# Layer 1 of a two-layer kernel: the experts' weighted biases for four token tiles at once, on four 32-row parts of TensorE

## The chip, the cores and the metric

The kernel runs on one core of one Trainium2 chip. The metric is the time of one execution in device microseconds (us). A core has five engines that work side by side, each through its own queue of instructions: TensorE (PE, with its weight loads listed as PEld), VectorE (DVE), ScalarE (ACT), GpSimd (POOL), and SyncE (SP), which here only starts DMA transfers. They hand work to each other through semaphores. Matmul results land in PSUM, eight banks of 128 partitions by 512 fp32 numbers, from which DVE and ACT read them; everything else lies in SBUF.

## The reference, cut to what matters

Eight sequences of 512 tokens with 256 features go through two layers. Layer 0 (a recurrent attention and a mixture of experts that takes one expert per token) isn't touched by the change. Layer 1 is a softmax attention with 16 heads, then a mixture in which every token goes through all eight experts:

```python
gate_logits = jax.nn.softmax(x @ gate_w + gate_b, axis=-1)
selected = (gate_logits >= THRESHOLD).astype(x.dtype)
weights = gate_logits * selected
wsum = jnp.sum(weights, axis=-1, keepdims=True)
weights = weights / jnp.where(wsum == 0, jnp.ones_like(wsum), wsum)
for e in range(E):
    out = out + weights[:, e:e + 1] * (x @ expert_w[e] + expert_b[e])
```

The sum over `e` of `weights[:, e] * expert_b[e]` is a small matrix product by itself: the weights of a token (8 numbers) times the table of biases (8 by 256). This is the "weighted bias" of which the change speaks. The result, times a gate row, is added to `x`.

## The kernel before, in words

Layer 1 works batch by batch. A batch has NT = 4 token tiles of 128 tokens. The main loop of layer 1 counts steps `n`, 16 per batch: four groups of heads (`c`) times four query tiles (`i`). A step does three things for attention. `scores` makes the scores of four heads: four matmuls on 32 rows each, each into a PSUM bank of its own (line 1419); VectorE adds the position bias and takes the lowest value (line 1428), ScalarE takes the exponential (line 1433). `turn`, four steps behind, transposes the probabilities of four heads through TensorE (line 1445) and copies them back, two with VectorE (line 1454) and two with ScalarE (line 1452). `weigh`, one step further behind, multiplies them with the values (line 1466), adding up in one bank that is held for four steps.

All else is cut into pieces that are put into a list `side` with a place each, counted in steps, and are issued between the steps when their place has come. `prologue` (the norm of the next batch, its transposes on line 179 and its projections, lines 240 and 257) and `tail` (all that follows attention for the batch before) make such pieces. A `tail` begins six steps into the next batch. Its pieces, with their places counted from there: `heads_out`, `heads_T`, `project` (lines 1492, 1507, 1518) for the four tiles, then `statistics` at 6.6, the transposed norm and the gate's logits (line 1542) from 7.6, `weights` at 14 (the softmax over eight gates and the threshold, for all four tiles in one go), `weights_T` at 15.4, and `experts(i)` at 17, 18.9, 20.8 and 22.7. The tail of a batch thus reaches into the second batch after it. The last tile of the last batch but one is put off to 30.8, into the tail of the last batch.

`weights_T` transposes the weights of the four tiles (128 by 8 each) with four transposes into one bank (line 1576), and VectorE copies the 8 by 512 result into `wT` (line 1578). `experts(i)` starts with the weighted bias of its tile: one matmul with 8 rows (line 1584; an fp32 matmul shows as two instructions in the trace), copied by ScalarE into the accumulator `acc` (line 1586). Then come four pairs of experts, two fp32 matmuls into one bank for each pair (line 1590, sixteen instructions in all), from which VectorE adds `weight * result` to `acc`, expert by expert (line 1595). GpSimd multiplies with the gate row (line 1599; VectorE in the last batch) and starts the DMA that adds `acc` to the output (line 1600).

What is issued in what order: the pieces stand in the order in which the loop traces them, and the framework's planner places them at compile time. In the program before, TensorE's order in layer 1 is that of tracing but for four instructions out of some three thousand, which a later one passed because their input was not ready in the planner's reckoning; on VectorE and ScalarE it mixes more freely. `tc.issue_after(step)` keeps `turn`, `weigh` and the side pieces behind the step's score matmuls on TensorE. At run time each engine goes through its queue in that order and waits where an input or a buffer isn't ready. A PSUM tile gets the bank that was released longest ago; with one of the eight banks held by `weigh`, seven go round.

In SBUF the pool `layer1` ends at byte 115,328 of a partition and the next one in use begins at 116,800. The table of biases, `eb`, is loaded by SP in layer 0, in `load1`.

Of the kernel before, what the change touches and what calls it, by code (L numbers as in the profile page):

```python
# [11 lines left out]
F32 = mybir.dt.float32  # L12
U32 = mybir.dt.uint32
AF = mybir.ActivationFunctionType
ALU = mybir.AluOpType
# [4 lines left out]
P = 128  # L20
B = 8
S = 512
D = 256
NH = 16
HD = 16
NT = S // P
NE = 8
# [36 lines left out]
def tile_two_layers(ctx: ExitStack, tc: tile.TileContext, t: dict, out: bass.AP):  # L64
    nc = tc.nc
# [9 lines left out]
    def bank():  # L75
        n_ps[0] += 1
        return banks[0].tile([P, 512], F32, tag="ps", name=f"ps{n_ps[0]}")
# [17 lines left out]
    ident = cst[:, C_ID : C_ID + P]  # L95
# [57 lines left out]
    w1 = {}  # L153
# [124 lines left out]
    with ExitStack() as l0:  # L278
# [988 lines left out]
        def follow(i, qk, V):  # L1267


            x1, norms = [], []  # L1270
            _, pieces = attend(i, qk, V, x1, norms)
            work = {}

            def begin():
                work["route"] = route(i, x1, norms)
                next(work["route"])

            def more():
                next(work["route"])

            def settle():
                work["experts"] = experts(i, *next(work["route"]))
                next(work["experts"])

            def on():
                next(work["experts"])

            pieces += [(34, begin), (42, more), (51, more), (57, more), (60, more), (62, settle)]

            late, pace, starts = {  # L1290
                NT - 1: (0, 4, [10 * j for j in range(NSLOT)]),
                NT - 2: (14, 4.2, [43]),
                NT - 3: (11, 4.6, [8, 22, 37, 47]),
            }.get(i, (11, 4.6, [8, 22, 37, 47]))
            rest = []
            for j in range(NSLOT):
                for half in range(2):
                    if j < late:
                        pieces.append((68 + pace * (j + half / 2), on))
                    else:  # L1300
                        rest.append((starts[j - late] + 3 * half, on))
            if i == NT - 1:
                rest += [(200, on), (250, on)]

            at, apart = [(1, 2.2), (21, 2.2), (108, 7), (0, 0)][i]
            return pieces, rest, [
                (at + apart * n, on) for n in range(B + DEPTH[i])
            ]

        def load1():  # L1310

            early.close()
            wp1 = ctx.enter_context(tc.tile_pool(name="weights1", bufs=1, side="right"))

            def put(key, shape, src):
                w1[key] = wp1.tile(shape, F32, name=f"{key}1")
                nc.sync.dma_start(w1[key], src)

            put("wqkv", [P, 2, 3 * D], t["W_attnT"].rearrange("(k p) m -> p k m", p=P))
            put("bqk", [P, 4], t["b_qk"])  # L1320
            put("bv", [P, D], t["b_v"].partition_broadcast(P))
            w1["strips"] = wp1.tile([P, NH, S], F32, name="strips1")
            put("wp", [P, 2, D], t["W_projT"].rearrange("(k p) m -> p k m", p=P))
            put("bp", [P, D], t["b_proj"].partition_broadcast(P))
            put("gw", [P, 2, NE], t["gate_w1"].rearrange("(k p) e -> p k e", p=P))
            put("gbias", [P, NE], t["gate_b1"].partition_broadcast(P))
            put("eb", [NE, D], t["expert_b"])

            w1["xs"] = wp1.tile([P, NT, D], F32, name="xs_first")

# [26 lines left out]
        for i in range(NT):  # L1357
# [23 lines left out]
            if i + 1 < NT:  # L1381
                parts, more, _ = front(i + 1, 47 if i > 0 else 30)
                pieces = pieces + more + (later if i == 0 else [])
            run(pieces, scan(i, before["K"], before["V"]))
        more, last, _ = follow(NT - 1, before["qk"], before["V"])
# [18 lines left out]
    with ExitStack() as l1:  # L1404
        lp = l1.enter_context(tc.tile_pool(name="layer1", bufs=2))

        strips, wp, bp = (w1[key] for key in ("strips", "wp", "bp"))
        gw, gbias, eb, ew = (w1[key] for key in ("gw", "gbias", "eb", "ew"))

        def scores(b, c, i):  # L1410


            kT, qT, prs = got[b]["kT"], got[b]["qT"], got[b].setdefault(c, {})
            g, o = c // 2, c % 2
            W = (i + 1) * P
            pscs = [bank() for _ in range(4)]
            for r in range(4):
                rows = slice(32 * r, 32 * r + 32)
                made = nc.tensor.matmul(  # L1419
                    pscs[r][:, :W], qT[rows, g, o, i * P : (i + 1) * P], kT[rows, g, :W],  # L1420
                    start=True, stop=True,
                )
            for r in range(4):
                n = 8 * g + 2 * r + o

                sc = lp.tile([P, S], F32, tag="sc", name=f"sc{b}_{i}_{n}", bufs=4)
                low = lp.tile([P, 1], F32, tag="low", name=f"low{b}_{i}_{n}", bufs=8)
                nc.vector.tensor_tensor_reduce(  # L1428
                    out=sc[:, :W], in0=pscs[r][:, :W], in1=strips[:, n, S - W :],
                    scale=1.0, scalar=3.0e38, op0=ALU.add, op1=ALU.min, accum_out=low,  # L1430
                )
                pr = lp.tile([P, W], F32, tag=f"pr{i}", name=f"pr{b}_{i}_{n}", bufs=6)
                nc.scalar.activation(pr, sc[:, :W], AF.Exp, bias=low, scale=-1.0)  # L1433
                prs[r, i] = pr
            return made.ins
# [40 lines left out]
        def tail(b, got):  # L1476
# [3 lines left out]
            g11 = spread(lp, "g11", b)  # L1480
            hT = []
            lg = lp.tile([P, NT, NE], F32, tag="lgd", name=f"lgd{b}")
            wt = lp.tile([P, NT, NE], F32, tag="wtd", name=f"wtd{b}")

            ys, yTt, stats, wTs = {}, {}, {}, []

            def heads_out(i):

# [59 lines left out]
            def weights():  # L1548
                def row4(name):
                    return lp.tile([P, NT], F32, tag=name, name=f"{name}{b}")  # L1550

                def wide(x):
                    return x.unsqueeze(2).to_broadcast([P, NT, NE])

                top = row4("topd")
                nc.vector.tensor_reduce(top, lg, AX.X, ALU.max)
                nc.vector.tensor_sub(lg, lg, wide(top))
                nc.scalar.activation(lg, lg, AF.Exp)
                tot = row4("totd")
                nc.vector.tensor_reduce(tot, lg, AX.X, ALU.add)  # L1560
                nc.vector.reciprocal(tot, tot)
                nc.vector.tensor_mul(lg, lg, wide(tot))
                nc.vector.scalar_tensor_tensor(
                    wt.rearrange("p i e -> p (i e)"), lg.rearrange("p i e -> p (i e)"), 0.1,
                    lg.rearrange("p i e -> p (i e)"), ALU.is_ge, ALU.mult,
                )
                ws = row4("wsd")
                nc.vector.tensor_reduce(ws, wt, AX.X, ALU.add)
                nc.vector.scalar_tensor_tensor(ws, ws, 0.0, ws, ALU.is_equal, ALU.add)
                nc.vector.reciprocal(ws, ws)  # L1570
                nc.vector.tensor_mul(wt, wt, wide(ws))

            def weights_T():
                pt = bank()
                for i in range(NT):
                    nc.tensor.transpose(pt[:NE, i * P : (i + 1) * P], wt[:, i, :], ident)
                wT = lp.tile([NE, S], F32, tag="wT", name=f"wT{b}", bufs=1)
                nc.vector.tensor_copy(wT, pt[:NE, :])
                wTs.append(wT)

            def experts(i):
                cols = slice(i * P, (i + 1) * P)
                pb = bank()
                nc.tensor.matmul(pb[:, :D], wTs[0][:, cols], eb, start=True, stop=True)  # L1584
                acc = lp.tile([P, D], F32, tag="accd", name=f"accd{b}_{i}")
                nc.scalar.copy(acc, pb[:, :D])
                for e in range(0, NE, 2):
                    pe = bank()
                    for k in range(2):
                        nc.tensor.matmul(  # L1590
                            pe, hT[0][:, k, cols], ew[:, k, e : e + 2, :],
                            start=(k == 0), stop=(k == 1),
                        )
                    for j in range(2):
                        nc.vector.scalar_tensor_tensor(  # L1595
                            acc, pe[:, j * D : (j + 1) * D], wt[:, i, e + j : e + j + 1], acc,
                            ALU.mult, ALU.add,
                        )
                (nc.vector if b == B - 1 else nc.gpsimd).tensor_mul(acc, acc, g11)  # L1599
                nc.gpsimd.dma_start(y2d[b][i], acc, accum_op=ALU.add)  # L1600
# [21 lines left out]
        for n in range(B * STEP + NT + 1):  # L1622
            b, m = divmod(n, STEP)
# [23 lines left out]
            with tc.issue_after(step):  # L1647
                last, turned = turned, None
                if NT <= n < B * STEP + NT:
                    b, m = divmod(n - NT, STEP)  # L1650
# [110 lines left out]
```

## Time and profile before

| what | us |
|---|---|
| median of 3 runs (lowest, highest) | 2216.25 (2212.28, 2221.45) |
| the profiled execution, and its span from first to last instruction | 2215.8, 2214.1 |
| TensorE busy (share of the span) | 1718.3 (78%) |
| VectorE busy | 1580.6 (71%) |
| ScalarE busy | 1081.1 (49%) |
| GpSimd busy | 642.1 (29%) |
| bias matmuls, line 1584: 64 instructions, busy | 23.0 |
| expert matmuls, line 1590: 512 instructions, busy | 232.6 |
| weight transposes, line 1576: 32 instructions of 0.27 each | first at 1518.7, last at 2175.9 |
| copies of the bias into the accumulator, line 1586: 32, mean | 0.37 |
| copy of the transposed weights, line 1578: 8, mean | 0.68 |
| mean granted TensorE clock over the span (1 is full speed) | 0.874 |

Layer 0 fills the span to about 1360 us, layer 1 the rest. Busy times of matmuls overlap, since several are in the array at once: where it matters what a group of matmuls costs, the distance from its first issue to the issue of the next group says more than the duration of its instructions.

### The profile page before, as it was taken

How to read it: one execution, taken by the hardware profiler on the slowest of the kernel's cores; microseconds unless marked ns; L12 is line 12 of the kernel's file. 1: busy time of each engine (PE TensorE's matmuls, PEld its weight loads, DVE VectorE, ACT ScalarE, POOL GpSimd, SP SyncE). 2: the span in 40 equal slices, each digit the busy share in tenths (PEclk: the TensorE clock that was granted, in tenths of full speed). 3: DMA queues.
4: the chain of work that ended last, by engine and by line, in shares of the span. 5: the costliest groups of instructions: out<-in, count | busy, mean ns of one | idle time of the engine just before them, and what ended most of it. 6: DMA issues, size and time to landing. Idle time of an engine off the chain costs nothing. (4 is left out here: it accounts for less than half of the span.)

```text
span 2214.1 us, 32513 instructions
## 1 busy us (share of the span) xinstructions
PE 1718.3 (78%) x10906; PEld 1196.4 (54%) x10906; DVE 1580.6 (71%) x4523; ACT 1081.1 (49%) x2674; POOL 642.1 (29%) x920
## 2 busy tenths in 40 slices
PE   5342056479686796839995898999999999999988
PEld 4221035259574695728874786555555555555544
DVE  5999998969989699899753004677676666676754
ACT  4253035555366553623342336886666574747421
POOL 1313013355254553543463643010111101010210
PEclk8666566689897898969997999999999999999998
DMA  5110000358103582128765883000101010000101
GB/s 165 49 50 5 0 1 11 99 209 313 33 13 108 198 311 72 38 90 303 234 110 153 272 275 72 1 20 8 27 13 25 13 22 13 22 20 6 23 17 12
DMA packets 88630, 189.58 MB, mean 86 GB/s; under 512 B 13688, under 2 KB 67104, under 8 KB 75664
## 3 DMA queue, kind: packets, MB, share of 16 engines
q0 software_dynamic: 33696, 137.43, 19.3%
q1 hardware_dynamic: 54768, 50.09, 7.9%
q8 instruction: 86, 1.41, 0.3%
q14 instruction: 80, 0.66, 0.1%
HBM read 175.10 MB, written 36.93 MB: 96 GB/s over the span
## 5 line engine op out<-in xcount | busy, mean ns | idle before, releaser
L1433 ACT ACTIVATE pr<-sc,low 128x384 f32<-128x384 f32 (+3 forms) x512 | 255.6, 556 | 196.3 <-DVE low L1428 193.2
L1428 DVE CUSTOM_DVE_ANT_0 sc<-ps,strips 128x384 f32<-128x384 f32 (+3 forms) x512 | 225.6, 486 | 87.2 <-PE ps L1419 55.6
L1190 PE MATMUL ps<-hTs,w 128*128 128x128 f32 x1920 | 239.4, 286 | 14.0 <-DMA w<-in_wrows,idx 9.0
L1190 PEld LDWEIGHTS ps<-hTs,w 128*128 128x128 f32 x1920 | 235.5, 201 | 21.4 <-issue 11.6
L745 DVE TENSOR_REDUCE state<-terms 128x16 f32<-128x272 f32 x512 | 227.3, 444 | 15.6
L756 DVE TENSOR_TENSOR state<-state,upd 128x256 f32<-128x256 f32 x511 | 222.2, 435 | 14.9
L1590 PE MATMUL ps<-ew,hTd 128*128 128x512 f32 x512 | 232.6, 608 | 0.0
L1209 PE MATMUL ps<-w,act 128*128 128x256 f32 x960 | 223.7, 387 | 6.5 <-DMA w<-in_wrows,idx 4.0
L741 DVE TENSOR_TENSOR terms<-state,K 128x256 f32<-128x256 f32 x512 | 216.3, 422 | 14.9
L751 DVE TENSOR_TENSOR upd<-K,state 128x256 f32<-128x256 f32 x511 | 214.4, 420 | 16.1
L1199 ACT ACTIVATE act<-ps,w 128x128 f32<-128x128 f32 x480 | 137.3, 370 | 135.4 <-PE ps L1190 122.2
L1445 PE MATMUL ps<-cst,pr 128*128 128x128 f32 x1280 | 189.9, 292 | 15.3 <-DVE low L1428 12.0
L1209 PEld LDWEIGHTS ps<-w,act 128*128 128x128 f32 x960 | 182.0, 195 | 31.4 <-issue 4.0
L1595 DVE SCALAR_TENSOR_TENSOR accd<-ps,wtd,accd 128x256 f32<-128x256 f32 x256 | 123.7, 483 | 100.7 <-PE ps L1590 86.6
L1445 PEld LDWEIGHTS ps<-cst,pr 128*128 128x128 f32 x1280 | 147.2, 147 | 84.8 <-DVE low L1428 24.1
L1599 POOL TENSOR_TENSOR accd<-accd,bc_g 128x256 f32<-128x256 f32 x28 | 20.4, 728 | 545.6 <-DVE accd L1595 545.6
L1145 POOL DMA_INDIRECT w<-in_wrows,idx x120 | 124.2, 1035 | 184.1 <-ACT act L1199 58.8
L1590 PEld LDWEIGHTS ps<-ew,hTd 128*128 128x128 f32 x512 | 96.3, 193 | 120.5 <-issue 106.4
L1419 PE MATMUL ps<-kT,qTc 32*128 32x128 f32 (+3 forms) x1024 | 132.1, 491 | 4.4 <-DVE low L1428 2.6
L1454 DVE COPY prT<-ps 128x512 f32<-128x512 f32 (+3 forms) x256 | 117.0, 484 | 8.9 <-PE ps L1445 8.5
L1452 ACT COPY prT<-ps 128x512 f32<-128x512 f32 (+3 forms) x256 | 98.9, 414 | 7.2 <-PE ps L1445 6.6
L1165 PE MATMUL ps<-cst,hslot 128*128 128x128 f32 x120 | 24.7, 290 | 98.2 <-DMA hslot<-hs 71.3
(296 smaller groups left out, 2956.3 us busy)
## 6 DMA issues: line engine op xcount, KB each, us to landing
hs<-zero SPq DMA_DIRECT2D x4, 1920.0 KB
hslot<-hs SPq DMA_DIRECT2D x60, 128.0 KB
ys<-ysb POOLq DMA_DIRECT2D x60, 128.0 KB
x<-in_x SPq DMA_DIRECT2D x32, 128.0 KB
strips<-strip_d SPq DMA_DIRECT2D x16, 256.0 KB
out<-accd POOLq DMA_DIRECT2D x32, 128.0 KB
wm<-in_wmod SPq DMA_DIRECT2D x4, 768.0 KB
xt<-in_x SPq DMA_DIRECT2D x12, 256.0 KB
```

The source lines that it names most:

```text
L741: nc.vector.tensor_mul(term[:, :, :HD], M, K[:, s, :].unsqueeze(1).to_broadcast([P, HD, HD]))
L745: nc.vector.tensor_reduce(delta, term, AX.X, ALU.add)
L751: nc.vector.tensor_mul(upd, K[:, s, :].unsqueeze(2).to_broadcast([P, HD, HD]), delta.unsqueeze(1).to_broadcast([P, HD, HD]),)
L756: yield nc.vector.tensor_sub(M, M, upd).ins
L1190: nc.tensor.matmul(ph[:, q * P : (q + 1) * P], w[:, k * FF + f * P : k * FF + (f + 1) * P], hT[:, k, :], start=(k == 0), stop=(k == 1),)
L1199: nc.scalar.activation(act[:, f, :], ph[:, q * P : (q + 1) * P], AF.Relu, bias=w[:, 2 * FF + f : 2 * FF + f + 1],)
L1209: nc.tensor.matmul(py[:, :D], act[:, f, :], w[:, f * D : (f + 1) * D], start=(f == 0), stop=(f == NFC - 1),)
L1419: made = nc.tensor.matmul(pscs[r][:, :W], qT[rows, g, o, i * P : (i + 1) * P], kT[rows, g, :W], start=True, stop=True,)
L1428: nc.vector.tensor_tensor_reduce(out=sc[:, :W], in0=pscs[r][:, :W], in1=strips[:, n, S - W :], scale=1.0, scalar=3.0e38, op0=ALU.add, op1= ...
L1433: nc.scalar.activation(pr, sc[:, :W], AF.Exp, bias=low, scale=-1.0)
L1445: nc.tensor.transpose(pt[:, (i - j) * P : (i - j + 1) * P], prs[r, i][:, j * P : (j + 1) * P], ident,)
L1590: nc.tensor.matmul(pe, hT[0][:, k, cols], ew[:, k, e : e + 2, :], start=(k == 0), stop=(k == 1),)
```

## The change

The four tiles' weights now lie in one tile of SBUF of 128 tokens by 4 by 32, tile `i` in columns 32i to 32i+7, the other columns zero. There are two such tiles, used in turn by even and odd batches; GpSimd sets them to zero once, at the beginning of layer 1. One transpose of the whole 128 by 128 square puts tile `i`'s weights on partitions 32i to 32i+7. The table of biases is loaded four times, onto the same partitions. The four bias matmuls then read four different 32-row parts of the array and write four banks; they and ScalarE's four copies into accumulators move from `experts` into `weights_T`, so that a batch's four accumulators exist from there on (four slots instead of two). The two operations of `weights` that worked on flat rows of 32 numbers now work on 4 by 8 numbers at a stride of 32; their element counts are the same.

```diff
-            put("eb", [NE, D], t["expert_b"])
+            w1["eb"] = wp1.tile([P, D], F32, name="eb1")
+            for i in range(NT):
+                nc.sync.dma_start(w1["eb"][32 * i : 32 * i + NE, :], t["expert_b"])
...
+        wts = []
+        for k in range(2):
+            wts.append(lp.tile([P, NT, 32], F32, name=f"wtd{k}", bufs=1))
+            nc.gpsimd.memset(wts[k], 0.0)
...
-            wt = lp.tile([P, NT, NE], F32, tag="wtd", name=f"wtd{b}")
+            wt = wts[b % 2][:, :, :NE]
...
-                nc.vector.scalar_tensor_tensor(
-                    wt.rearrange("p i e -> p (i e)"), lg.rearrange("p i e -> p (i e)"), 0.1,
-                    lg.rearrange("p i e -> p (i e)"), ALU.is_ge, ALU.mult,
-                )
+                nc.vector.scalar_tensor_tensor(wt, lg, 0.1, lg, ALU.is_ge, ALU.mult)
...
             def weights_T():
                 pt = bank()
+                nc.tensor.transpose(
+                    pt[:, :P], wts[b % 2].rearrange("p i e -> p (i e)"), ident
+                )
+                wT = lp.tile([P, P], F32, tag="wT", name=f"wT{b}", bufs=1)
+                nc.vector.tensor_copy(wT, pt[:, :P])
+                pbs = [bank() for _ in range(NT)]
                 for i in range(NT):
-                    nc.tensor.transpose(pt[:NE, i * P : (i + 1) * P], wt[:, i, :], ident)
-                wT = lp.tile([NE, S], F32, tag="wT", name=f"wT{b}", bufs=1)
-                nc.vector.tensor_copy(wT, pt[:NE, :])
-                wTs.append(wT)
+                    rows = slice(32 * i, 32 * i + NE)
+                    nc.tensor.matmul(
+                        pbs[i][:, :D], wT[rows, :], eb[rows, :], start=True, stop=True
+                    )
+                for i in range(NT):
+                    acc = lp.tile([P, D], F32, tag="accd", name=f"accd{b}_{i}", bufs=4)
+                    nc.scalar.copy(acc, pbs[i][:, :D])
+                    accs.append(acc)
 
             def experts(i):
                 cols = slice(i * P, (i + 1) * P)
-                pb = bank()
-                nc.tensor.matmul(pb[:, :D], wTs[0][:, cols], eb, start=True, stop=True)
-                acc = lp.tile([P, D], F32, tag="accd", name=f"accd{b}_{i}")
-                nc.scalar.copy(acc, pb[:, :D])
+                acc = accs[i]
                 for e in range(0, NE, 2):
```

More of the change, by code (lines that the diff above doesn't have):

```diff
@@ L1482, in tail @@
             lg = lp.tile([P, NT, NE], F32, tag="lgd", name=f"lgd{b}")
-            wt = lp.tile([P, NT, NE], F32, tag="wtd", name=f"wtd{b}")
-            ys, yTt, stats, wTs = {}, {}, {}, []
+            wt = wts[b % 2][:, :, :NE]
+            ys, yTt, stats, accs = {}, {}, {}, []
             def heads_out(i):
```

## The prediction

> **What bounds the kernel now.** I read the page first, for the shape of the run. TensorE's row climbs to 9s in the right third; that is layer 1, the only place the change touches.
>
> ```profile
> PE   5342056479686796839995898999999999999988
> ```
>
> Then busy time by stretch, one stretch per batch of layer 1, cut at the first weight transpose of each batch (columns: length, then busy us and count of PE, PEld, DVE, ACT, POOL, then the granted clock).
>
> ```profile
> 1727.00:1832.50 105.50, 103.26 (x600) 56.77 (x596) 71.06 (x248) 64.16 (x142) 12.23 (x16) 0.97 0.09 18
> 1936.20:2037.80 101.60, 100.39 (x601) 54.89 (x598) 68.99 (x238) 60.53 (x137) 12.25 (x16) 1.00 0.07 14
> ```
>
> TensorE is busy 98% of a batch, VectorE 67%, ScalarE 61%. Equal work took 101.6 us at clock 1.00 and 105.5 at 0.97: throttling is worth up to 4 us a batch, and comes and goes.
>
> "Busy" does not say that a removed matmul shortens anything, so I took the timeline of the weight loads, which shows when each group is issued (columns: start, length, line, tiles, form, count, idle time before it and who ended it).
>
> ```profile
> 1726.97 0.31 PEld L1576 LDWEIGHTS ps<-cst,wtd 128*8 128x8 f32 x4 [0.84 <-DVE prT L1454]
> 1727.50 0.31 PEld L1419 LDWEIGHTS ps<-kT,qTc 32*128 32x128 f32 x8 [0.22 <-DVE prT L1454]
> ...
> 1731.61 0.29 PEld L1419 LDWEIGHTS ps<-kT,qTc 32*128 32x128 f32 x2 [0.36 <-ACT prT L1452]
> ...
> 1733.81 0.29 PEld L1584 LDWEIGHTS ps<-eb,wT 8*128 8x128 f32 x2 [0.41 <-DVE low L1428]
> 1734.43 0.30 PEld L1590 LDWEIGHTS ps<-ew,hTd 128*128 128x128 f32 x2 [0.33 <-DVE low L1428]
> ...
> 1745.77 0.36 PEld L1507 LDWEIGHTS ps<-cst,yc 128*128 128x128 f32 x2
> 1746.10 0.47 PEld L1492 LDWEIGHTS ps<-cst,yTc 128*128 128x128 f32 x4
> 1746.73 0.29 PEld L1584 LDWEIGHTS ps<-eb,wT 8*128 8x128 f32 x2 [0.17 <-ACT xnc L172]
> 1747.36 0.30 PEld L1590 LDWEIGHTS ps<-ew,hTd 128*128 128x128 f32 x2 [0.33 <-DVE rinvc L1495]
> ...
> 1754.42 0.31 PEld L1419 LDWEIGHTS ps<-kT,qTc 32*128 32x128 f32 x8 [0.76 <-DVE accd L1595]
> 1755.06 1.29 PEld L1445 LDWEIGHTS ps<-cst,pr 128*128 128x128 f32 x12 [0.33 <-issue]
> ...
> 1764.98 0.36 PEld L1507 LDWEIGHTS ps<-cst,yc 128*128 128x128 f32 x2
> 1765.51 0.29 PEld L1584 LDWEIGHTS ps<-eb,wT 8*128 8x128 f32 x2 [0.17 <-issue]
> ```
>
> A bias matmul (L1584) holds the issue for 0.62 us (1746.73 to 1747.36) and the interval is the same in every batch of the loop: it waits for nothing. The eight loads of a score step (four heads on 32 rows each, two passes, 128x256) take 0.64 us (1754.42 to 1755.06), no more than the two of one bias. And two 128x128 transposes take 0.33 us before another group of that form (1745.77 to 1746.10) but 0.53 before a bias (1764.98 to 1765.51): the change of form costs 0.2 more.
>
> The end of the kernel has experts alone:
>
> ```profile
> 2184.61 0.69 PE L1584 MATMUL ps<-eb,wT 8*128 8x256 f32 x2
> 2185.24 7.13 PE L1590 MATMUL ps<-ew,hTd 128*128 128x512 f32 x16
> 2192.30 0.69 PE L1584 MATMUL ps<-eb,wT 8*128 8x256 f32 x2
> ```
>
> A tile there lasts 7.69 us, of which sixteen expert matmuls at their spacing of 0.43 are 6.83; the bias costs 0.86 with its changes of form.
>
> Last, who can take up the moved work: ScalarE and VectorE where the biases go (one line of VectorE, then ScalarE).
>
> ```profile
> 1727.61 0.68 DVE L1578 COPY wT<-ps 8x512 f32<-8x512 f32 x1 [0.40 <-PE ps L1576]
> ...
> 1726.84 0.84 ACT L1452 COPY prT<-ps 128x384 f32<-128x384 f32 x2
> 1729.16 2.14 ACT L1433 ACTIVATE pr<-sc,low 128x384 f32<-128x384 f32 x4 [1.48 <-DVE low L1428]
> 1731.21 0.62 ACT L1452 COPY prT<-ps 128x256 f32<-128x256 f32 x2
> ```
>
> ScalarE is idle 1.48 us there, VectorE waits for TensorE.
>
> **What the Trainium skill says.** "TensorEngine Tiling (Array Packing)", Key Properties: tiles of the array run independently, and changing the tiling mode drains the engine. The trace agrees on both (0.64 for eight loads; 0.2 at a change). The same page, Gotcha 1 (PSUM Pressure): different row tiles write different PSUM banks. So the four biases need four banks at once. "TensorE: Matmul & The Clock Gate", Part 1: after an idle window of about 3.4 us the clock halves, the window running freely; the stretches above (0.97 against 1.00) fit. The same page, Architectural detail: ScalarE and VectorE take their instructions strictly in order, so the four copies delay what is traced behind them; the trace before shows nothing against it.
>
> **The change, part by part.** Batches 0 to 5 first, whose biases lie in the loop.
>
> *Removed, tiles 1 to 3.* Tile 1 follows L1492, tile 2 L1507, tile 3 L240 (issued 1780.77, the bias 1781.83: 1.06, against 0.76 for L240 before another 128x128 group). All are 128x128 like the experts, so the bias's 0.62 goes and the change before it too: 0.62+0.2, 0.62+0.2, 0.62+0.3 = 2.6 us.
>
> *Weights and tile 0.* Before, from the transposes to the first expert: 1726.97 to 1734.43 = 7.46 us, 0.53 of it four transposes, 0.62 tile 0's bias, and 0.55 a stall of the fourth score matmul on ScalarE (the 1731.61 line). After: one transpose (0.27), VectorE's copy of 128x128 (0.28, the row of that form in L1454, instead of 0.68), two hand-overs of some 0.05: the biases issue at +0.66. That is a **new wait** on TensorE of about 0.4. Queued behind it are the next score step and the transposes of probabilities; VectorE's next score reductions wait for those. If the planner puts the score step ahead of the biases, the wait is filled; take it as not filled. The biases cost about 0.5 (the score step's 0.64 less the change of form, as scores follow in the same form): scores start at +1.15, against +0.53.
>
> *Banks.* Seven of eight rotate, one holds sums. Transpose and biases take five, so the fourth score matmul waits for ScalarE's first copy (0.37, the L1586 row): bias done at +1.4, copy at +1.8. So scores end 0.86 later at +2.7 against +1.39 before, and the probability transposes (8 at 0.107, and a change) at +3.8 against +2.6: 1.2 late. Then the stall on ScalarE at 1731.61 takes up the delay. It ends when the four exponentials and one copy end, and these begin with the first score's reduction. Before, that began at 1728.56, 1.06 after the scores were issued, and VectorE had waited 0.27 for TensorE, not for its own copy; so it now comes 0.62 late, and the second score step too. With tile 0's bias of 0.62 gone, the first expert starts where it did, at 7.46: gain 0. Bounds: no wait binds, -1.2 (the 0.53 and 0.62 removed and 0.8 of stalls against 0.27 and 0.5 added); ScalarE's copies (4 x 0.37 = 1.5, less 0.5 that fits before the exponentials) fall ahead of work that TensorE waits for, +1.0.
>
> Per batch 2.6, six batches: **15.6 us**. Later in the batch ScalarE is saturated for some 20 us (softmax of the gates), but its work there is started by TensorE's projections, so an earlier start carries through.
>
> *Batch 6* (after the loop): transposes 2118.80, first bias 2120.16, first expert 2121.07 at the half clock. Biases at once cost what the first bias did; tiles 1 and 2 save 0.8 each; tile 3's bias at 2164.01 fills a wait for ScalarE and saves nothing: **1.5 us**.
>
> *Batch 7*: tiles 1 to 3, 3 x 0.86 = 2.6. From the transposes (2175.55) to the first expert (2177.55) one short transpose and copy instead of four and 0.68 save about 0.7; the expert work before it, freed of the filler, 0.5: **3.8 us**. Its fourth accumulator reuses the slot of the postponed tile of batch 6, whose output leaves at 2178.36; it is needed after 2199.
>
> *At nothing.* Three more bias loads on SP, 0.38 us each like the one at 927.41, before a gap of SP to 985.62; uncovered they would cost 1.2 us. Two memsets on POOL, no row shows one; POOL has nothing to do for 90 us at the beginning of layer 1 (its longest wait for `z`), and uncovered I bound them by the 0.73 of a POOL product each. The gate operations on rows of 32 instead of 8 keep their element counts (0.19). Four slots for accumulators: the copies then wait for no earlier output, which landed long before.
>
> Sum: 15.6+1.5+3.8 = 21 us. The profiled execution took 2215.8 us, span 2214.1 (1.7 around it, unchanged): 2194.8. It stands 0.45 below the median 2216.25, so the median goes to **2195 us**, 0.95% faster.
>
> **Rivals.** *The gain is half eaten.* The four biases do not overlap (8 x 0.21 + 0.2 = 1.9 us instead of 0.5: 1.4 per batch, 9 in all), or the new wait and banks cost the upper bound (+1.0, 6 in all). For it: TensorE already has waits on VectorE and ScalarE here. Against: 32-row scores do overlap. Time 2203, 2210 if both.
>
> *Slower: TensorE stands at the packed biases.* In each batch the four banks come free only after the next scores' reductions, and the copies stand behind four exponentials: 4 x 0.55 + 2.14 + 1.5 = 5.8 us, and the idle window halves the clock (2 us, half the difference of the two stretches): up to 7.8. It decides from 21/7 = 3.0 us a batch, and is slower by over 0.5% from 32/7 = 4.6. At 5.5: 2195+38 = 2233. Against: ScalarE's 1.48 us of idle time lie just where the copies fall due.
>
> *More: the clock.* Phases shift against the free-running window; if all batches ran like the 101.6 one (2 us less than the mean of 103.8 over the five stretches from transpose to transpose), 12 more: 2183.
>
> **How the numbers follow.** Measurement tells about 0.5% (11 us) from no change. Forecast 0.68, its own range 2187 to 2203; half eaten 0.20; slower 0.08; more 0.04. The range of 8 in 10 is 2184 to 2210: forecast, the clock's 2183 nearly, most of the half eaten. Faster (below 2205): 0.68+0.04+0.05 of the half eaten = 0.77; same 0.15; slower 0.08.
>
> **What would show it.** Expert groups of tiles 1 to 3 following L1492, L1507 and L240 with no L1584 between, 0.8 to 0.9 us earlier each; last tiles 6.85 us apart; eight L1584 loads within about 0.1 us per pass; ScalarE's copies in fours before the exponentials. Wrong if the L1584 groups spread over 2 us, if the stretch from transpose to first expert grows beyond 8.5 us, or if batches without throttling last over 101 us.

## The result, and the profile after

The changed kernel takes 2203.73 us (median of 10 runs, 2198.83 to 2208.69); the kernel before, beside it on the same chip, 2219.8 (10 runs, 2211.95 to 2228.84). The ratio is 0.9928, with an interval of 0.991 to 0.9947: 0.72% faster, 16 us, where 21 were forecast. The time forecast, 2195, was 8.7 too low: 5 of it are gain that did not come, and 3.6 are the kernel before, which stood at 2219.8 here and at 2216.25 in the runs that the forecast started from.

The profiled execution took 2204.43 us, with a span of 2202.7 and a mean clock of 0.877. In the page's second part TensorE's row ends as before, in 9s and 8s:

```profile
PE   5343047469687696848985888999999999999988
```

Busy time by stretch of the kernel after: first two batches cut at the weight transpose, as in the prediction, then the loop of layer 1 (first score step to last) and the tail (last score step to the end). The columns are those of the prediction, with the busy share of the DMA engines and their GB/s at the end.

```profile
1729.60:1834.50 104.90, 102.01 (x597) 57.58 (x593) 70.66 (x248) 64.29 (x143) 12.23 (x16) 0.95 0.09 18
...
1934.90:2034.20 99.30, 97.43 (x596) 53.86 (x593) 68.35 (x238) 60.33 (x137) 12.25 (x16) 1.00 0.08 14
...
1366.60:2097.10 730.50, 707.61 (x4374) 397.53 (x4374) 510.71 (x1825) 477.86 (x1053) 83.73 (x111) 0.97 0.10 20
2097.10:2202.70 105.60, 88.04 (x333) 45.97 (x332) 52.30 (x142) 23.15 (x57) 15.72 (x20) 0.89 0.11 16
```

And the loop and the tail of the kernel before:

```profile
1361.00:2102.80 741.80, 722.68 (x4392) 401.07 (x4392) 513.66 (x1825) 477.99 (x1053) 83.30 (x109) 0.98 0.09 19
2102.80:2214.10 111.30, 93.94 (x339) 48.16 (x338) 53.08 (x142) 23.64 (x57) 15.72 (x20) 0.90 0.10 15
```

The loop is 11.3 shorter and the tail 5.7. Batch 4 (the second line here and in the prediction), at clock 1.00 in both profiles, takes 99.35 us from transpose to transpose instead of 101.58: 2.2 less. The work of VectorE, ScalarE and GpSimd is nearly what it was (VectorE has 3 us less in the loop). Layer 0 ends at 1366.6 instead of 1361.0; the experiments below put its end between 1358.4 and 1371.7, also among kernels with the same layer 0, so this difference is scatter, and layer 1 is what to compare.

Now one batch, in the timeline of weight loads of the kernel after (start, length, line, tiles, form, count, idle time before it and who ended it). Lines 1581, 1589 and 1603 are now the transpose, the biases and the experts, 1427 the scores, 1453 the transposes of probabilities.

```profile
1729.64 0.14 PEld L1581 LDWEIGHTS ps<-cst,wtd 128*128 128x128 f32 x1 [0.84 <-DVE prT L1462]
1730.35 0.31 PEld L1589 LDWEIGHTS ps<-eb,wT 8*128 8x128 f32 x8 [0.57 <-DVE wT L1585]
1730.67 0.42 PEld L1427 LDWEIGHTS ps<-kT,qTc 32*128 32x128 f32 x6
1731.51 0.29 PEld L1427 LDWEIGHTS ps<-kT,qTc 32*128 32x128 f32 x2 [0.42 <-ACT accd L1594]
1732.34 0.86 PEld L1453 LDWEIGHTS ps<-cst,pr 128*128 128x128 f32 x8 [0.55 <-ACT accd L1594]
...
1735.93 0.31 PEld L1453 LDWEIGHTS ps<-cst,pr 128*128 128x128 f32 x3 [0.76 <-DVE yc L1505]
1736.76 0.14 PEld L1453 LDWEIGHTS ps<-cst,pr 128*128 128x128 f32 x1 [0.51 <-DVE low L1436]
1737.58 0.30 PEld L1603 LDWEIGHTS ps<-ew,hTd 128*128 128x128 f32 x2 [0.41 <-DVE low L1436]
...
1748.92 0.36 PEld L1515 LDWEIGHTS ps<-cst,yc 128*128 128x128 f32 x2
1749.24 0.47 PEld L1500 LDWEIGHTS ps<-cst,yTc 128*128 128x128 f32 x4
1749.68 0.30 PEld L1603 LDWEIGHTS ps<-ew,hTd 128*128 128x128 f32 x2
...
1767.32 0.36 PEld L1515 LDWEIGHTS ps<-cst,yc 128*128 128x128 f32 x2
1767.64 0.30 PEld L1603 LDWEIGHTS ps<-ew,hTd 128*128 128x128 f32 x2
```

Three things are to be seen. The eight loads of four biases hold the issue for 0.32 us together (1730.35 to 1730.67), half of what one bias of two loads took before (0.62). Tiles 1 and 2 start directly behind the transposes of line 1500 and 1515, with no idle time and no change of form. And the first expert comes 7.94 after the transpose (1729.64 to 1737.58), where it came after 7.46 before; just ahead of it the last transpose of probabilities waits 0.51 for VectorE's score reduction, a wait that the kernel before did not have.

ScalarE in the kernel after, from the same stretch:

```profile
1731.08 1.20 ACT L1594 COPY accd<-ps 128x256 f32<-128x256 f32 x4 [0.73 <-PE ps L1589]
1732.44 2.14 ACT L1441 ACTIVATE pr<-sc,low 128x384 f32<-128x384 f32 x4 [0.16 <-DVE low L1436]
```

The four copies stand together ahead of the four exponentials, end 0.16 before these can start, and so hold up nothing on ScalarE here.

### The profile page after: what moved, and what is told of

Its sections match the earlier page's. It is cut to its first block, busy times and chain, and to the rows that moved or that the text cites. A ratio compares the mean times of both kernels' runs of the same rounds, so it can differ in the third digit from the quotient of the medians.

```text
span 2202.7 us, 32510 instructions
## 1 busy us (share of the span) xinstructions
PE 1693.7 (77%) x10882; PEld 1187.5 (54%) x10882; DVE 1579.2 (72%) x4523; ACT 1080.6 (49%) x2674; POOL 642.2 (29%) x922
## 5 line engine op out<-in xcount | busy, mean ns | idle before, releaser
L1436 DVE CUSTOM_DVE_ANT_0 sc<-ps,strips 128x384 f32<-128x384 f32 (+3 forms) x512 | 225.5, 486 | 94.4 <-PE ps L1427 63.6
L745 DVE TENSOR_REDUCE state<-terms 128x16 f32<-128x272 f32 x512 | 227.3, 444 | 15.6
```

Source lines behind the costliest of these rows:

```text
L745: nc.vector.tensor_reduce(delta, term, AX.X, ALU.add)
L1436: nc.vector.tensor_tensor_reduce(out=sc[:, :W], in0=pscs[r][:, :W], in1=strips[:, n, S - W :], scale=1.0, scalar=3.0e38, op0=ALU.add, op1= ...
```

## The experiments

The ratio is to the kernel before, measured beside each kernel on the same chip, with its 95% interval. The columns behind it come from one profile of each kernel. "To first expert" is from the weight transpose to the first expert's load; "tiles 0 to 3" from the first load of tile 0 to that of tile 3 of the same batch, which holds the gain of tiles 1 to 3; both are those of batches 0 to 4, which hardly differ (the exceptions: tiles 0 to 3 took 48.27 in batch 4 of the kernel before and 48.43 in one batch of "biases late"). "Half clock" is the time in the loop at which half the clock was granted (0.5 in the profile's record of the clock).

| kernel | median us (runs) | ratio, interval | loop | tail | to first expert | tiles 0 to 3 | half clock |
|---|---|---|---|---|---|---|---|
| before | 2219.8 to 2221.6 | 1 | 741.8 | 111.3 | 7.46 | 48.02 | 34.1 |
| changed | 2203.73 (10) | 0.9928, 0.991 to 0.9947 | 730.5 | 105.7 | 7.95 | 45.45 | 37.5 |
| changed, second | 2199.26 (6) | 0.9919, 0.9887 to 0.995 | 729.4 | 104.0 | 7.95 | 45.45 | 37.7 |
| changed, third | 2200.41 (5) | 0.9907, 0.9892 to 0.9923 | 732.1 | 106.4 | 7.95 | 45.45 | 41.0 |
| biases late | 2211.35 (20) | 0.996, 0.9943 to 0.9976 | 740.5 | 106.4 | 8.51 to 8.87 | 45.45 | 47.8 |
| a step later | 2200.63 (6) | 0.9918, 0.9894 to 0.9943 | 731.4 | 105.2 | 7.22 | 45.45 | 47.9 |
| moved, full array | 2215.61 (20) | 0.9983, 0.9964 to 1.0001 | 749.6 | 107.1 | 8.94 | 45.45 | 64.9 |
| in place, 32 rows | 2219.24 (20) | 0.999, 0.9976 to 1.0005 | 739.1 | 110.9 | 7.19 | 48.02 | 30.7 |
| in place, full array | 2201.16 (7) | 0.9914, 0.9888 to 0.994 | 732.1 | 104.6 | 6.92 | 46.82 | 37.5 |
| no biases | 2182.12 (4) | 0.9828, 0.9787 to 0.9868 | 720.6 | 97.7 | see below | 45.45 | 37.5 |
| tail alone | 2200.65 (6) | 0.9912, 0.9892 to 0.9932 | 730.5 | 100.7 | 7.95 | 45.45 | 34.1 |
| step and tail | 2201.37 (6) | 0.9902, 0.9884 to 0.992 | 731.5 | 101.2 | 7.22 | 45.45 | 48.0 |

### The changed kernel twice more

No edit; two further measurements, beside the other kernels.

> The changed kernel once more, beside the others on the same chip. Theory of the prediction, corrected by the trace (the gain is issue time of TensorE: three expert tiles start 0.83, 0.82 and 0.93 us earlier each; the first expert 0.49 later): ratio to before 0.991 to 0.995; first expert 7.95 us after the weight transpose in every batch of the loop, last expert tile 53.4. Rival (the clock's free window made the gain): these two distances vary from run to run by more than 0.5 us.

> The changed kernel beside these two on one chip, for the comparison: ratio 0.991 to 0.994; distances 7.95 and 45.45 us from the transpose to the first and from the first to the last expert tile, 104 to 106 us from the last score step to the end.

Ratios 0.9919 and 0.9907 agree with 0.9928. The stretches inside a batch, 7.95 and 45.45, are the same in all three. What varies between executions is layer 0, by 8 us in these three, and the parts of the loop in which the windows at half clock fall: from the first score step to the first transpose 157.5, 157.9 and 162.7 us, and from tile 3 of a batch to the next transpose 45.9 to 51.7. On the mean of the three profiles the loop is 730.7 (11.1 less than before), the tail 105.4 (5.9 less), layer 1 836.0 (17.1 less). The kernel before has one profile only, of an execution 4 us below its median.

### The two halves of the change apart

The biases can be done one at a time where they were, from the one transpose:

```diff
             def weights_T():
...
-                pbs = [bank() for _ in range(NT)]
...
+                held.append(wT)
             def experts(i):
-                acc = accs[i]
+                rows = slice(32 * i, 32 * i + NE)
+                pb = bank()
+                nc.tensor.matmul(pb[:, :D], held[0][rows, :], eb[rows, :], start=True, stop=True)
+                acc = lp.tile([P, D], F32, tag="accd", name=f"accd{b}_{i}", bufs=2)
+                nc.scalar.copy(acc, pb[:, :D])
```

> One transpose of the square and biases on their own 32-row parts, but each bias stays at the head of its expert tile. Theory: tiles 12.92, 18.78 and 16.33 us apart as before, first expert at about 7.1 us (three transposes less, 0.32), last tiles 7.69 apart; 2 to 3 us faster than before in all, ratio 0.998 to 1.0. Rival (the one transpose, or other banks, makes most of the gain): 8 us faster or more.

The single transpose is worth 0.27 us a batch (7.46 to 7.19 to the first expert), and the time, 0.999, can't be told from that before. The gain is in the biases, not in the transpose.

The other half: moved and in one place, but each bias on all 128 rows of the array, so that the four can't run side by side.

```diff
+            nc.gpsimd.memset(w1["eb"], 0.0)
...
-                    rows = slice(32 * i, 32 * i + NE)
-                    nc.tensor.matmul(
-                        pbs[i][:, :D], wT[rows, :], eb[rows, :], start=True, stop=True
-                    )
+                    nc.tensor.matmul(pbs[i][:, :D], wT, eb, start=True, stop=True)
```

> The biases moved as in the change, but each matmul works on all 128 rows (so each sums all four tiles' biases, which is not what the reference asks). Theory (overlap on 32-row parts carries the moved biases): eight passes of 0.21 in a row, 1.7 us and 0.2 for the change of form, against 0.32: first expert at 9.0 to 9.6 us, tiles 1 to 3 as in the changed kernel, 7 to 10 us slower than that: ratio about 0.996. Rival (the biases' own time is hidden there by other waits): first expert at 8.0, time as the changed kernel.

The weight loads of this kernel around one transpose:

```profile
1740.27 0.14 PEld L1582 LDWEIGHTS ps<-cst,wtd 128*128 128x128 f32 x1 [0.84 <-DVE prT L1463]
1740.98 1.59 PEld L1589 LDWEIGHTS ps<-eb,wT 128*128 128x128 f32 x8 [0.57 <-DVE wT L1586]
1742.90 0.31 PEld L1428 LDWEIGHTS ps<-kT,qTc 32*128 32x128 f32 x8 [0.33 <-PE ps L1589]
...
1747.01 0.29 PEld L1428 LDWEIGHTS ps<-kT,qTc 32*128 32x128 f32 x2 [0.36 <-ACT prT L1461]
...
1748.06 0.42 PEld L1454 LDWEIGHTS ps<-cst,pr 128*128 128x128 f32 x4 [0.76 <-DVE yc L1506]
1749.21 0.30 PEld L1601 LDWEIGHTS ps<-ew,hTd 128*128 128x128 f32 x2 [0.41 <-DVE low L1437]
```

One after another the four biases hold the issue for 1.92 us (1740.98 to 1742.90) instead of 0.32. Nearly all of the gain is gone: 0.9983, an interval that reaches 1. So the biases do overlap on their 32-row parts in the changed kernel, and without the overlap the move doesn't pay. But not all of the loss is that stretch: 1.60 us more of biases make the first expert 0.99 later, 6 us in six batches, while its median stands 12 above the changed kernel's first one and 16 above its second, taken beside it (7 to 10 were expected). Its profile (one of its longer executions, 2226.42 us) shows more time at half clock, 64.9 us in the loop, and its five stretches from tile 3 to the next transpose add up to 251.2 us, against 239.6 to 242.7 in the changed kernel's three profiles. Why the half clock grew isn't shown.

A detail is needed below. Here the first step's four scores run without a wait (the 1742.90 line, eight loads in one group), while in the changed kernel the fourth one waits for ScalarE's first copy (its 1731.51 line). The second step's fourth score waits for ScalarE's copy of probabilities (the 1747.01 line), as it did in the kernel before, and the four transposes of probabilities behind it run without a break (the 1748.06 line, four in one group).

### Where the biases stand

Packed and all four, but ahead of tile 0's experts, where tile 0's bias was:

```diff
+                held.append(wT)
+            def biases():
+                wT = held[0]
                 pbs = [bank() for _ in range(NT)]
...
             def experts(i):
+                if i == 0:
+                    biases()
```

> The transpose and VectorE's copy stay at 15.4, the four packed biases and their copies come just ahead of the first expert tile's matmuls. Theory: TensorE no longer waits for the copy, no score step stands behind the biases; 7.46 before, less 0.3 for three transposes, so first expert at 7.1 us, 0.85 less than in the changed kernel, 5 us less over six batches: ratio 0.989 to 0.991. Rival (banks): the expert matmuls wait for banks until ScalarE has copied behind its exponentials, the first tile lasts 1 to 2 us longer than 6.5 and the time is that of the changed kernel or more.

```profile
1736.93 0.64 PEld L1595 LDWEIGHTS ps<-eb,wT 8*128 8x128 f32 x4 [0.41 <-DVE low L1436]
1737.89 0.65 PEld L1595 LDWEIGHTS ps<-eb,wT 8*128 8x128 f32 x4 [0.32 <-DVE low L1436]
1738.87 0.30 PEld L1611 LDWEIGHTS ps<-ew,hTd 128*128 128x128 f32 x2 [0.33 <-issue]
```

In this timeline of weight loads the biases are torn in two, since the third waits for a bank that a score reduction still holds (it starts at 1737.89; VectorE's fourth reduction ends at 1737.83), and their form changes both ahead of them and behind: 1.94 us from the first to the expert. The expectation, 7.1 to the first expert, was wrong; it is 8.51 to 8.87, and half of the gain in time is lost (0.996). Free banks decided here where four biases at once could stand.

One step later than in the change, behind the next score step:

```diff
...
             yield 15.4, weights_T
+            yield 16.4, biases
```

> The packed biases one step later than the transpose (place 16.4). Theory that the new wait of TensorE for VectorE's copy (0.44 us) counts in full: first expert at 7.5 us, ratio 0.990. Rival (ScalarE): the four copies now fall behind exponentials of 384 columns, the fourth score matmul of the next step waits for them, first expert at 8 to 9 us, slower than the changed kernel by 0 to 6 us.

```profile
1726.62 0.14 PEld L1583 LDWEIGHTS ps<-cst,wtd 128*128 128x128 f32 x1 [0.84 <-DVE prT L1462]
...
1730.29 0.32 PEld L1595 LDWEIGHTS ps<-eb,wT 8*128 8x128 f32 x6 [0.17 <-DVE prT L1462]
1730.98 0.18 PEld L1595 LDWEIGHTS ps<-eb,wT 8*128 8x128 f32 x1 [0.36 <-ACT prT L1460]
...
1733.84 0.30 PEld L1609 LDWEIGHTS ps<-ew,hTd 128*128 128x128 f32 x2 [0.41 <-DVE low L1436]
```

The scores fill the wait for the transposed weights, and the first expert comes 7.22 after the transpose, 0.73 sooner than in the change (7.5 was expected). The fourth bias now has the wait on ScalarE that the fourth score had. Yet the time is the same, 0.9918 against 0.9919 beside it (0.990 was expected). In its profile the loop has 47.9 us at half clock instead of 37.5 to 41.0, and the five stretches from tile 3 to the next transpose add up to 246.1 us instead of 239.6 to 242.7. Six times 0.73 are 4.4 us, and what came back as throttling is of that size; why this place draws more of it was not found.

### What a bias costs, and what is left

On all 128 rows and in place, so that nothing is moved and no form changes (the edit is against the kernel in place on 32 rows):

```diff
+            nc.gpsimd.memset(w1["eb"], 0.0)
...
-                nc.tensor.matmul(pb[:, :D], held[0][rows, :], eb[rows, :], start=True, stop=True)
+                nc.tensor.matmul(pb[:, :D], held[0], eb, start=True, stop=True)
```

> As the one before, but each bias works on all 128 rows (it sums all four tiles' biases, which is not what the reference asks), so that its form is that of the experts. Theory (a change of form costs 0.2 to 0.3): a bias costs 0.43 instead of 0.83: tiles 12.5, 18.4 and 15.8 us apart, last tiles 7.26 apart, 8 to 12 us faster than before, ratio 0.995. Rival (the form costs nothing, the bias its 0.62): tiles as before, ratio 0.999.

```profile
1738.88 0.30 PEld L1594 LDWEIGHTS ps<-eb,wT 128*128 128x128 f32 x2 [0.41 <-DVE low L1437]
1739.23 0.38 PEld L1600 LDWEIGHTS ps<-ew,hTd 128*128 128x128 f32 x2
...
1751.41 0.30 PEld L1594 LDWEIGHTS ps<-eb,wT 128*128 128x128 f32 x2
1751.74 0.41 PEld L1600 LDWEIGHTS ps<-ew,hTd 128*128 128x128 f32 x2
```

With the experts' form on both sides, the expert's loads follow the bias's after 0.33 to 0.35 us, and a bias lengthens the way from tile 0 to tile 1 by 0.41 (12.50 against 12.09 without one), where the 8-row bias lengthened it by 0.83 (12.92). The ratio is 0.9914, as that of the change, where 0.995 was expected. As it stands this kernel adds the biases of all four tiles to each. A usable form with the one transpose would need the biases of one tile at a time in a table that is zero elsewhere; for four tiles that is 4 KB of a partition, 3 more than the table has in the kernel before, where 1.5 KB is free between the pools; so it was not built. Another form would keep the layout before, weights of 8 by 512 and one table, and fill both with zeros up to 128 rows; by the sizes of the tiles this takes no more bytes of a partition. It was not tried, so whether the move is needed at all for this gain stays open.

All weighted biases left out:

```diff
+                        if e + j == 0:
+                            nc.vector.tensor_scalar_mul(acc, part, gate)
+                        else:
+                            nc.vector.scalar_tensor_tensor(
+                                acc, part, gate, acc, ALU.mult, ALU.add
+                            )
...
-            yield 15.4, weights_T
```

> No weight transpose, no bias, no copies; the first expert's product starts the accumulator. The weighted biases are left out. Theory: tiles 12.09, 17.95 and 15.40 apart as in the changed kernel, which has nothing left of them there; what the moved work still costs is the rest, 1 to 1.8 us a batch: 7 to 12 us faster than the changed kernel, ratio 0.987 to 0.990. Rival (the moved work is hidden): within 3 us of the changed kernel.

Its loop and its tail:

```profile
1365.30:2085.90 720.60, 702.62 (x4319) 392.97 (x4319) 508.24 (x1820) 470.39 (x1029) 84.02 (x112) 0.97 0.10 20
2085.90:2183.60 97.70, 83.57 (x315) 44.27 (x314) 51.58 (x140) 20.69 (x49) 15.69 (x20) 0.92 0.12 17
```

Layer 1 takes 818.3 us. So the biases with their transposes and waits cost 34.8 us before (853.1), and the change took half of it; 18 are left. Ten of these are in the loop, where the first expert comes 1.64 us a batch sooner from the same place in the score step (six times that are 9.8), and 8 in the tail. That is more than the 7 to 12 that were expected.

### The tail

In the kernel after, TensorE waits in batch 6 for the last operation of the gate weights:

```profile
2109.86 0.86 PE L1474 MATMUL ps<-prT,v 128*32 128x256 f32 x16
2113.09 0.30 PE L1581 MATMUL ps<-cst,wtd 128*128 128x128 f32 x1 [2.37 <-DVE wtd L1576]
...
2166.92 0.27 PE L1581 MATMUL ps<-cst,wtd 128*128 128x128 f32 x1
2167.86 0.71 PE L1589 MATMUL ps<-eb,wT 8*128 8x256 f32 x8 [0.67 <-DVE wT L1585]
2168.50 27.73 PE L1603 MATMUL ps<-ew,hTd 128*128 128x512 f32 x64
```

An expert matmul doesn't need the transposed weights; only the accumulation on VectorE does. So for batches 6 and 7 two pairs of tile 0's experts were put ahead of the transpose, in two kernels: with the biases otherwise where the change has them, and with the biases a step later.

```diff
+            late = b >= B - 2
             def experts(i):
+                ahead = {}
+                if late and i == 0:
+                    ahead[0] = pair(0)
+                    ahead[2] = pair(2)
+                    weights_T()
+                    biases()
...
+                    pe = ahead.pop(e) if e in ahead else pair(e)
```

> The changed kernel, but in batches 6 and 7 two pairs of the first tile's experts are issued ahead of the weight transpose, so that TensorE has work while the weights and the copy are made. Theory (in the last two batches TensorE waits for the weights: the kernel without biases lost 7 us less there): 3 to 5 us off the stretch from the last score step to the end (104 to 106 us in the changed kernel), the loop unchanged; ratio 0.989 to 0.991. Rival (that gain was the biases' own time): under 1.5 us.

> The same, and in batches 0 to 5 the packed biases one step later than the transpose. Theory: first expert at 7.22 instead of 7.95 us in six batches, and 3 to 5 us off the end: 7 to 9 us less than the changed kernel, ratio 0.988. Rival (what a later step saves is given back at the half clock in the softmax stretch, as in the kernel with only the later step): time of the kernel with the changed tail alone.

Batch 6 in the second of the two:

```profile
2116.03 0.86 PE L1474 MATMUL ps<-prT,v 128*32 128x256 f32 x16
2116.82 3.70 PE L1611 MATMUL ps<-ew,hTd 128*128 128x512 f32 x8
2120.36 0.27 PE L1583 MATMUL ps<-cst,wtd 128*128 128x128 f32 x1
```

Eight expert matmuls fill the wait, and the tail lasts 100.7 and 101.2 us, where the change has 104.0 to 106.4: the 3 to 5 us that were expected are in the profiles. The times do not show them: 0.9912 and 0.9902, beside 0.9907 for the changed kernel on the same chip, with intervals of 0.003 to 0.004, and medians of 2200.65 and 2201.37 beside 2200.41. The 7 to 9 us expected of the second kernel did not come; its loop has 48.0 us at half clock. A version that surely beats the change was not found.

## Why the prediction was right, and where it was off

The time, 2203.73, lies within the range of 8 in 10, but just above the forecast's own (2187 to 2203) and inside that of "half eaten". Of the 0.95% forecast 0.72 came.

**The mechanism, tiles 1 to 3: right.** 0.62 and 0.2, 0.2 and 0.3 were worked out. The distance from one tile to the next fell from 12.92 to 12.09, 18.78 to 17.96 and 16.32 to 15.40: 0.83, 0.82 and 0.92, together 2.57 against 2.6. In batch 4 it was 2.82 (48.27 to 45.45), in the last batch of the loop 2.27 (43.82 to 41.55).

**Weights and tile 0: this step failed.** Gain 0 was put down, with a loss of 1.0 as the bound; the loss was 0.49, from 7.46 to 7.95. Up to the second score step it went as worked out: biases at +0.71 (0.66), scores at +1.03 (1.15), the first step's fourth score waiting for ScalarE's first copy until +1.87 (1.8), scores' end at +2.70 (2.7), end of the transposes at +3.7 (3.8), the fourth score of the second step 0.61 later than before (0.62). The stall on ScalarE took up the delay there, and that stall is gone from the profile after.

What failed is that this stall was counted as slack. It held up the fourth score alone. The first score of the second step comes 1.15 late, and VectorE's first reduction of that step follows it, 1.27 behind in both kernels. Before (the loads of the scores, then the reduction):

```profile
1730.91 0.33 PEld L1419 LDWEIGHTS ps<-kT,qTc 32*128 32x128 f32 x6 [0.17 <-DVE prT L1454]
...
1732.18 0.69 DVE L1428 CUSTOM_DVE_ANT_0 sc<-ps,strips 128x512 f32<-128x512 f32 x1 [0.34 <-PE ps L1419]
```

And after:

```profile
1734.73 0.44 PEld L1427 LDWEIGHTS ps<-kT,qTc 32*128 32x128 f32 x8 [0.17 <-DVE prT L1462]
...
1736.00 0.69 DVE L1436 CUSTOM_DVE_ANT_0 sc<-ps,strips 128x512 f32<-128x512 f32 x1 [0.44 <-PE ps L1427]
```

The last of the four transposes of probabilities behind these scores needs the bank that this reduction frees. Before, the stall at the fourth score kept the transposes back until that bank was free. After, they come without the stall, and the last one waits for the reduction instead, 0.51 in each of the six batches (the 1736.76 line, "DVE low L1436"). Whichever of the two waits comes last, the way from the second step's first score to the first expert is the same: 3.52 before, 2.90 of it without tile 0's bias of 0.62, and 2.85 after. So the 1.15 went through, less the bias of 0.62 and these 0.05: 0.48, and 0.49 was measured. The kernel with the moved biases on the full array supports it: there the stall on ScalarE is back and the wait for VectorE is not, and the way is 2.89. (That 1.60 us more of biases cost only 0.99 there has another reason: the first step's fourth score no longer waits for a copy, and the second step's first score is only 0.95 later.)

**The sum.**

| | forecast | measured, three profiles |
|---|---|---|
| tiles 1 to 3, six batches | -15.6 | -15.4 |
| weights and tile 0, six batches | 0 | +2.6 |
| the rest of the loop | 0 | +1.7 |
| batches 6 and 7 | -5.3 | -5.9 (-4.9 to -7.3) |
| layer 1 | -21 | -17.1 |

The last batch of the loop lost only 0.14 to its first expert (7.81 to 7.95), hence 2.6 and not 2.9. Nearly all of the rest is one stretch of one profile, the 162.7 us from the first score step to the first transpose where the other two have 157.5 and 157.9 and the kernel before 157.8; it has 24 us at half clock there, the others 14. The stretches from tile 3 to the next transpose add up to 241.4 before and on the mean of the three after.

**The bias at 0.5, the batches without throttling, the tail: right in the main.** The four took 0.32 and not 0.5, the batches at clock 1.00 stayed below 101 us, the last tiles run through without a gap (64 expert matmuls from 2168.50 on, 27.73 us, 6.9 a tile). The sum of the tail came out by luck, since its parts were off on both sides. From the transpose of batch 6 to that of batch 7 it gained 2.2 to 4.5 us instead of 2.0: tile 3's bias, which was to save nothing, alone saved 1.5 (22.18 to 20.67 from tile 2). From there to the end it gained 2.8 instead of 3.3. Nothing showed of what was put at nothing. Layer 0, which has the loads, varies by more between executions of one kernel; the memsets stand at the beginning of layer 1, and the way from there to the first transpose hasn't grown in two of three profiles (157.5 and 157.9, against 157.8).

**The clock: two readings that don't hold.** The two stretches that the prediction called equal work are not: the one at clock 1.00 has 10 instructions fewer on VectorE and 5 on ScalarE, and in the profile after, where both batches 3 and 4 ran at clock 1.00, they took 100.4 and 99.3 us. So some 1 us of the 3.9 between the two isn't the clock. Nor does an idle window stand ahead of the half clock. In batches 0 to 4 of the profile before and the three of the changed kernel there are 16 stretches at half clock; in the 3.4 us ahead of each, TensorE was by the profile busy for 2.2 to 2.9 us and idle for no more than 0.56 at a time. What does bring the half clock about isn't shown.

**The rivals.** "Half eaten" has the time (2203 to 2210 was its span, 2203.73 the result), and half of its second cause: the new waits cost half the upper bound. Its first cause, no overlap, is refuted by the 0.32 us of the four biases; the moved kernel on the full array shows what it would have been, 1.92 and a ratio of 0.9983. "Slower" needed 3.0 us a batch lost; the loss was 0.49, and the copies ended ahead of the exponentials. "More: the clock" didn't come: the half clock held for 37.5 to 41.0 us of the loop, against 34.1 before.

## What to carry to other kernels

When a stall is said to take up a delay, look for work of other engines that hangs on something ahead of the stall: it comes late in full, and may be the next wait. A small matmul in a stream of large ones costs its change of form on both sides, so first see what it costs in the form of its neighbours (on all 128 rows, with zeros), before it is moved to stand among others of its kind. Moving pays for small matmuls that overlap; packed, these four cost less than one alone, and one after another they gave the gain back.

## What was not expected of the hardware

- A bias with 8 rows of contraction costs 0.83 us between matmuls on the full array, and one with all 128 rows 0.41. The Trainium skill, "TensorEngine Tiling (Array Packing)", Key Properties, says that a change of tiling mode drains the engine; the runs fit that, and the difference, 0.42, is half of what the small bias costs.
- Four packed biases (eight passes, 8x256) held the issue for 0.32 us where scores in the same form followed, and scores alone, before a group on the full array, for 0.64.
- The clock was halved without an idle window: 16 times after 3.4 us in which TensorE was idle for no more than 0.56 us at a time.
- Where the biases stood later than in the change, the loop had some 48 us at half clock, in one profile of each of the three kernels that had them so; four profiles with the biases where the change has them have 34.1 to 41.0. The cause is open.
